# Four edges to a partition instead of three in a graph layer, with places found per load, degrees earlier and chunk sums in free order

## The chip, the cores and the metric

The kernel runs on one core of a Trainium2 chip. The metric is the time of one execution in microseconds (us) on the device; the times shown are of three runs and one further, profiled execution. The engines are named as the profile names them: PE is TensorE (PEld its weight loads), DVE is VectorE, ACT is ScalarE, POOL is GpSimd, SP is SyncE, which here only issues transfers.

## The reference

There are 625 nodes with 512 features and 20,625 edges sorted by destination: 10,000 random ones in both directions and a self loop for each node. Each edge has one of four types and a weight. With layer norms whose gains are applied where named:

```python
h   = maximum(layernorm(x), 0)
msg = sum over r of (h[src] @ W_rel[r] + b_rel[r]) * where(type == r, weight, 0)
agg = segment_sum(msg, dst) / maximum(segment_sum(weight, dst), 1)
x1  = layer_norm(h + h @ W_self + b_self + agg, ln1)
ffn = gelu(x1 @ W_ffn1 + b_ffn1) @ W_ffn2 + b_ffn2       # 512 -> 1024 -> 512
out = x + layer_norm(x1 + ffn, ln2)
```

## The kernel before, in words

The nodes are cut into five blocks of 125. A *table* of 20 chunks, one for each relation and block, holds `h[block] @ W_rel[r]` and, in its 126th row, the relation's bias row; it lies in device memory, and the last nine chunks also stay on chip (`kept`). Blocks 0 to 2 (`OUTER`, the dense blocks) and blocks 3 and 4 (`inner`, the gathered blocks) add up their edges in two different ways.

**Dense blocks.** Every node's edges are consecutive, at most 64 of them (slots). The kernel finds, for each node, where they begin: it compares the first edge of each tile of 128 edges (`find_tiles`, L471), gathers a row of every fourth destination (`dst_4`, an indirect transfer issued by POOL for each block, `rows_of_tiles`, L477), counts in it (`find_windows`, L480) and gathers the 64-slot window (`win`). From the windows come the slots' weights (`slot_weights`, L496), the fields of a slot split into bf16 parts (`slot_fields`, L513), the degrees (`slot_degrees`, `relation_degrees`), and then, for 16 slots at a time (a *unit*, four to a block, twelve in all), one-hot matrices on DVE (`slot_hots`, L608). PE multiplies them into *banks* (`slot_sums`, L637), and DVE reduces each bank into `sums_w` (L643): for each node, a weight for each row of the table. PE then sums the 20 chunks of the table with these weights (`chunk_sum`, L1054); eleven chunks are loaded back, two to a transfer (`chunk_load`), into three buffers `tr`. Six units (`EARLY`) are made during the table's products, the others after them.

**Gathered blocks.** The edges of a part of the list are laid out three to a partition (`EG` = 3): group k holds 128 x 3 edges, and partition p has edges 3p, 3p + 1, 3p + 2 of it. POOL gathers the table row of every edge (`gather`, L931, 128 rows to a transfer) into eight buffers `ms`. ACT scales the first of the three by its weight (`first_row`, L939), DVE adds the others whose destination is the same node (`row_added`, L957), ACT and DVE split the sum in two fp32r parts (`high` L943, `low` L947), and PE adds both with a one-hot of the first edge's node (`edge_sum`, L977 and L978; the last group of a sum in fp32, L980). With EG = 3 there are 23 groups, 69 gathers. A node whose edges begin inside a partition has its first edges there counted apart (`first_edges`, L550, `first_columns`, L565): EG - 1 further gathers for each of the two blocks (`gather_first`, L985, `add_first`, L982).

**Order.** The first part (L815 to L902) has an order written out by hand: a double loop over relation r and block i, and in each turn four matmuls of table rows (`table_rows`, L367) and then the other steps at the turn in which an `if` names them. PE, DVE, ACT and POOL follow it; SP's transfers are placed by the framework, and `later_loads` (L232) gives the weights' loads after each relation. The second part is planned: each step has an engine, a duration, predecessors, buffers and a rank, and `Plan.times` (L103) simulates them and emits in that order. Once emitted, each engine goes strictly in order.

Table products run first, then the self products (`self_part`, L384), chunk sums and gathered sums, then the first norm of a block, its turn (L325), the up product with Gelu (L722, L726), the down product (L740) and the last norm with its store.

Of the kernel before, what the change touches and what calls it, by code (L numbers as in the profile page):

```python
# [14 lines left out]
ALU = mybir.AluOpType  # L15

P = 128
EG = 3
SLOTS = 64
# [119 lines left out]
def gnn_layer(ctx, tc, x, edges, edge_groups, firsts, fourths, windows, w_self, w_rel, w_ffn1, w_ffn2, brel_in, rows_in, bf1_in, out, n_edges):  # L139
# [12 lines left out]
    nc = tc.nc  # L152
# [304 lines left out]

    def before_node(out, of, n):

        nc.vector.tensor_tensor(found[:, :, :n], of, node_f.unsqueeze(2).to_broadcast([P, NB, n]), op=ALU.is_lt)
        nc.vector.reduce_sum(out, found[:, :, :n], axis=mybir.AxisListType.X)

# [11 lines left out]
    def rows_of_tiles(b0, b1):  # L477
        rows_of(fourths, at_i[:, 0, :], lambda b: dst_4[:, b, :], b0, b1)

    def find_windows():  # L480
        n = fourths.shape[1]
        nc.vector.tensor_copy(ends[:, :, :n], dst_4)
        before_node(before[:, 1, :], ends[:, :, :n], n)
        nc.vector.scalar_tensor_tensor(before[:, 1, :], at_f[:, 0, :], float(fourths.shape[1]), before[:, 1, :],
                                       op0=ALU.mult, op1=ALU.add)
        nc.vector.tensor_scalar(at_f[:, 1, :], before[:, 1, :], -1.0, 0.0, op0=ALU.add, op1=ALU.max)
        nc.vector.tensor_copy(at_i[:, 1, :], at_f[:, 1, :])
        rows_of(windows, at_i[:, 1, :], lambda b: win[:, b, :, :].rearrange("p f s -> p (f s)"))

# [106 lines left out]
    QT = 4  # L596
# [213 lines left out]
    CH = 2  # L810
    FIRST_AT = (2, 2)
    units = [(d, u) for d in range(ND) for u in range(SL // UNIT)]
    EARLY = 6
    PER_ROW = 3
    with tc.manual_schedule(engines={PE, DVE, ACT, mybir.EngineType.Pool}):  # L815
        nc.scalar.activation(gelu_of, ones, AF.Gelu)
# [18 lines left out]
        for r in range(R):  # L835
            for i in range(NB):
# [15 lines left out]
                if (r, i) == (0, 0):  # L852
                    rows_of_tiles(0, 2)
                    next_norm(3)
                    rows_of_tiles(2, 4)
                if (r, i) == (0, 1):
                    rows_of_tiles(4, NB)
                if (r, i) == (0, 3):
                    find_windows()
                if (r, i) == (1, 0):  # L860
                    edge_columns()
                    for n in range(NB):
                        nc.vector.tensor_add(xs[:, n, :], xs[:, n, :], b2_bc)
# [15 lines left out]
                if (r, i) == (1, NB - 1):  # L879
                    group_columns()  # L880
# [5 lines left out]
                if (r, i) == FIRST_AT:  # L886
                    first_edges()
                    load_first_edges()
# [6 lines left out]
            later_loads(r)  # L895
        assert not waiting
# [18 lines left out]

    own = {}
    for n, b in enumerate(ep.order):
        first, second, added = self_part(b)
        rank = (2, 0.1 * n) if n < len(OUTER) else (5, n)
        s = op("PE", 1.735, first, take=["ps"], rank=rank)  # L920
        s = op("PE", 1.735, second, after=[s], give=["T"], lag=0.25, rank=rank)
        own[b] = op("DVE", 0.68, added, after=[s], give=["ps"], rank=(0.6,) if b in OUTER else None)
# [130 lines left out]

    def chunk_sum(b, c, first, last):  # L1054
        if first:
            acc[b,] = ps_one.tile([P, D], F32, tag="one", name=f"acc{b}")
        nc.tensor.matmul(acc[b,], sums_w[b][:NG + 1, c, :], kept[(b, c) if (b, c) in kept else c][:NG + 1],  # L1057
                         start=first, stop=last)

# [19 lines left out]

    stay, i = list(range(NC - KEPT, NC)), 0  # L1080
    for d, b in enumerate(OUTER):
        weights_of(d)
        order = (*stay, *range(NC - KEPT))
        for c in order:
            if c not in stay and (b, c) not in here:
# [3 lines left out]
                here.update({(b, c + k): ld for k in range(n)})  # L1089
            first, last = m[b] is None, c == order[-1]  # L1090
            m[b] = op("PE", 0.87, lambda b=b, c=c, first=first, last=last: chunk_sum(b, c, first, last),
                      after=[m[b], here.get((b, c)), summed.get(d)], take=["one"] if first else [],
                      give=["tr"] if (b, c) in here and (c % CH == CH - 1 or c == NC - KEPT - 1) else [], lag=0.25,
                      rank=(2, 2 + 0.01 * i), level=4.4)
            if i == 8:
                t = op("PE", 0.1, lambda: total_outside(), after=[m[b]], take=["ps"], give=["ps"], lag=2.0, rank=(2, 2.085))
            if i == 16:
                op("PE", 0.1, read_outside, after=[t, m[b]], rank=(2, 2.165), level=0.45)
# [209 lines left out]
```

## Time and profile before

| | us |
|---|---|
| three runs | 262.32, 263.18, 266.7 |
| their median | 263.18 |
| profiled execution, time | 264.32 |
| profiled execution, span | 262.4 |
| PE busy | 248.7 (95% of the span) |
| DVE busy | 184.4 (70%) |
| POOL busy | 112.2 (43%) |
| ACT busy | 66.4 (25%) |
| mean transfer rate | 183 GB/s |

The span is what the trace shows from the first instruction to the last; the execution's own time lies 1.9 us above it. All positions below are us from the span's start. A busy PE is not PE at its peak, since the modelled ends of pipelined matmuls overlap the next; the distance from one matmul's start to the next tells more. A fp32 matmul of the source appears as two records. In a timeline, a bracket at a line's end says how long the engine sat idle before it and what ended the wait; "issue" means nothing that the profile shows. Three stretches follow one another: table products to 89, sums and self products to about 153, feed forward mixed with the last sums to 255.6, and then the last norm and store.

### The profile page before, as it was taken

What the parts mean: (1) busy time and instruction counts of PE and PEld (TensorE: products, weight loads), DVE (VectorE), ACT (ScalarE), POOL (GpSimd) and SP (SyncE); (2) the same over time, 40 slices, a digit from 0 to 9 for tenths busy, and PEclk for the clock granted to TensorE, in tenths of its full rate; (3) what the DMA queues carried; (4) which work ended last, traced back from release to release, by engine and by line L of the source; (5) the groups of instructions that cost most, each with busy time, mean ns of one, the idle gap of its engine ahead of it and who ended that gap; (6) DMA issues with size and microseconds to landing.
All of it is one profiled execution on the core that took longest, in us unless ns stands there. A gap on an engine that the chain in (4) does not pass through costs nothing.

```text
span 262.4 us, 3165 instructions
## 1 busy us (share of the span) xinstructions
PE 248.7 (95%) x1047; PEld 141.6 (54%) x1047; DVE 184.4 (70%) x388; ACT 66.4 (25%) x127; POOL 112.2 (43%) x156
## 2 busy tenths in 40 slices
PE   7999998969999999999999999999999999999990
PEld 3444443435555445444445577445559586685960
DVE  4460647699999899962799998697597792711414
ACT  3232111311122202131311043232444532140420
POOL 7163340000400028776876457877778750200100
PEclk9999999999999999999999999999999999999997
DMA  5948863967322287589895679979866651010101
GB/s 207 332 181 256 307 210 109 361 239 297 130 93 65 59 261 210 160 238 283 251 316 190 197 208 251 249 246 258 265 192 170 195 152 42 0 39 0 44 2 40
DMA packets 20259, 47.93 MB, mean 183 GB/s; under 512 B 2383, under 2 KB 3097, under 8 KB 20112
## 3 DMA queue, kind: packets, MB, share of 16 engines
q1 hardware_dynamic: 13636, 27.54, 32.0%
q0 software_dynamic: 6304, 19.89, 26.2%
q10 hardware_dynamic: 300, 0.26, 0.4%
q8 instruction: 9, 0.15, 0.2%
q14 instruction: 10, 0.08, 0.1%
HBM read 41.29 MB, written 6.52 MB: 182 GB/s over the span
## 4 chain that ended last, share of the span: by engine, by line
PE 61%; DVE 23%; DMA 9%; issue 2%; ACT 2%; SPq 1%; DVEq 0%; ACTq 0%
PE pt L372 17%; PE pu L722 14%; PE po L740 13%; PE acc L1057 9%; DVE sums_w L643 5%; DMA table<-m 5%; DVE high L626 4%; DVE low L620 3%; DMA ms<-table,row_i 3%; DVE ea L957 3%; PE bank L637 2%; PE acc L978 1%; DVE eq L623 1%; PE acc L977 1%; SPq L212 1%
## 5 line engine op out<-in xcount | busy, mean ns | idle before, releaser
L933 POOL DMA_INDIRECT ms<-table,row_i x69 | 72.1, 1046 | 52.1 <-DMA tr<-table 26.5
L372 PE MATMUL pt<-wr,hT 128*128 128x512 f32 x160 | 72.0, 599 | 0.0
L372 PEld LDWEIGHTS pt<-wr,hT 128*128 128x128 f32 x160 | 29.7, 193 | 32.0 <-issue 31.1
L722 PEld LDWEIGHTS pu<-x1T,w_sb 128*128 128x128 f32 x320 | 37.7, 192 | 3.4 <-issue 2.4
L722 PE MATMUL pu<-x1T,w_sb 128*128 128x125 f32 x320 | 38.2, 276 | 0.2 <-DVE sums_w L643 0.2
L957 DVE SCALAR_TENSOR_TENSOR ea<-ms,wgt_g,ea 128x512 f32<-128x512 f32 x43 | 31.8, 750 | 8.0 <-DMA ms<-table,row_i 7.6
L740 PE MATMUL po<-w_sb,gT 128*125 128x512 f32 (+2 forms) x96 | 36.0, 521 | 0.0
L1057 PE MATMUL acc<-tr,sums_w 126*128 126x512 f32 x66 | 30.7, 596 | 0.0
L643 DVE TENSOR_REDUCE sums_w<-bank 126x160 f32<-126x480 f32 x48 | 28.7, 651 | 0.8 <-PE bank L637 0.8
L380 ACT ACTIVATE m<-pt,rx 125x512 f32<-125x512 f32 x20 | 13.8, 688 | 57.8 <-PE pt L372 46.4
L939 ACT ACTIVATE ea<-ms,ed 128x512 f32<-128x512 f32 x23 | 15.9, 692 | 45.7 <-DMA ms<-table,row_i 27.4
L1057 PE MATMUL acc<-m,sums_w 126*128 126x512 f32 x54 | 25.7, 600 | 0.0
L726 ACT ACTIVATE gT<-pu,bf 128x125 f32<-128x125 f32 x40 | 14.4, 366 | 38.3 <-PE pu L722 38.3
L637 PEld LDWEIGHTS <-low 128*128 128x128 bf16 x192 | 15.8, 146 | 15.3 <-issue 15.1
L740 PEld LDWEIGHTS po<-w_sb,gT 128*125 128x125 f32 x96 | 16.4, 188 | 14.0 <-issue 11.6
L947 DVE TENSOR_TENSOR el<-ea,eh 128x512 fp32r<-128x512 f32 x20 | 13.6, 685 | 11.1 <-ACT eh L943 11.1
L637 PE MATMUL bank<-high,low 128*128 128x120 bf16 x192 | 15.9, 224 | 3.9 <-DVE sums_w L643 3.9
L943 ACT CAST eh<-ea 128x512 fp32r<-128x512 f32 x20 | 11.7, 584 | 27.3 <-DVE ea L957 24.4
L392 PE MATMUL pz<-ws_sb,hT 128*128 128x512 f32 x40 | 18.3, 596 | 0.0
L748 DVE TENSOR_TENSOR y<-po,z 125x512 f32<-125x512 f32 (+2 forms) x6 | 3.6, 600 | 20.6 <-PE po L740 20.6
L1057 PEld LDWEIGHTS acc<-tr,sums_w 126*128 126x128 f32 x66 | 12.1, 190 | 10.9 <-issue 10.5
L620 DVE TENSOR_TENSOR low<-turned,grid 128x2000 bf16<-128x2000 bf16 x12 | 14.3, 1193 | 3.1 <-ACT turned L606 3.1
(162 smaller groups left out, 232.5 us busy)
## 6 DMA issues: line engine op xcount, KB each, us to landing
tr<-table SPq DMA_DIRECT2D x15, 504.0 KB
table<-m SPq DMA_DIRECT2D x20, 250.0 KB
w_sb<-in_L_gnn_W_ffn_dram SPq DMA_DIRECT2D x2, 2048.0 KB
wr<-in_L_gnn_W_rel_dram SPq DMA_DIRECT2D x3, 1024.0 KB
ms<-table,row_i POOLq DMA_INDIRECT x69, 4.8
ws_sb<-in_L_gnn_W_self_dram SPq DMA_DIRECT2D x1, 1024.0 KB
rows<-in_rows_dram SPq DMA_DIRECT2D x1, 1024.0 KB
out_dram<-y SPq DMA_DIRECT2D x4, 224.0 KB
```

Source lines behind the costliest of these rows:

```text
L372: nc.tensor.matmul(p, hT[i][:, k, :], wr_sb[r][:, k, :], start=(k == 0), stop=(k == KD - 1))
L392: nc.tensor.matmul(p[0], hT[i][:, k, :], ws_sb[:, k, :], start=(k == 0), stop=(k == KD - 1))
L620: nc.vector.tensor_tensor(low[:, :, :NG, :], of[:, 0].rearrange("p (a t) -> p a t", t=TB).unsqueeze(2).to_broadcast([P, nb_, NG, TB]), gri ...
L637: nc.tensor.matmul(p[:, i * W:(i + 1) * W], low[:, t // TB, :, t % TB], high[:, t // TP, :, t % TP], start=True, stop=True)
L643: nc.vector.tensor_reduce(sums_w[OUTER[d]][:NG + 1, :, n0:n0 + 2 * QT].rearrange("p c (t h) -> p t h c", h=2), p[:NG + 1, :QT * 3 * 2 * NC ...
L722: nc.tensor.matmul(pu[:, :nn], w1_sb[:, k, f * P:(f + 1) * P], x1T_b()[:, k, :nn], start=(k == 0), stop=(k == KD - 1))
L726: nc.scalar.activation(box["gT"][:, f, :nn], pus[f][:, :nn], AF.Gelu, bias=bf1[:, f:f + 1])
L740: nc.tensor.matmul(po[h][:n, :w], box["gT"][:, f, at], w2_sb[:, f, c], start=(f == 0), stop=(f == KF - 1))
L933: nc.gpsimd.indirect_dma_start(out=ms[j], out_offset=None, in_=table[:, :], in_offset=bass.IndirectOffsetOnAxis(ap=row_i[:, j:j + 1], axis=0))
L939: nc.scalar.activation(box["sum"], ms[j], AF.Copy, scale=wgt[:, j:j + 1])
L957: nc.vector.scalar_tensor_tensor(to, ms[j], wgt_g[:, k, q - 1:q], box["sum"], op0=ALU.mult, op1=ALU.add)
L1057: nc.tensor.matmul(acc[b,], sums_w[b][:NG + 1, c, :], kept[(b, c) if (b, c) in kept else c][:NG + 1], start=first, stop=last)
```

## The change

`EG` becomes 4: 17 groups of four, 68 gathers, and three first-edge gathers for each gathered block. `find_windows` works on a range of blocks: the dense blocks' places are found in turn (0, 2) from their own `dst_4` rows, the others in (0, 3). The edge columns and the residual adds move to turn (0, 1) and (0, 3); slot weights and fields from (1, 1) to (0, 4); degrees from (2, 0) to (1, 0), group columns from (1, 4) to (1, 1), first edges from (2, 2) to (1, 2), so that all three stand ahead of the first one-hots, which start at (1, 3) instead of (1, 4). Seven units instead of six are made in this part. SP joins the engines that follow the written order, and the later loads are given by turn. In the second part the chunk sums of a block no longer form a chain: any chunk that is there may be next, and the last three self products get a level of their own.

```diff
-EG = 3
+EG = 4
...
-    def later_loads(r):
-        if r == 0:
-            load_wr(2)
+    def later_loads(r, i):
+        if (r, i) == (0, 0):
             bias_rows()
-        if r == 1:
-            load_wr(3)
+        if i == NB - 1 and r < R - 2:
+            load_wr(r + 2)
+        if (r, i) == (1, 2):
+            nc.sync.dma_start(bf1, bf1_in)
             nc.sync.dma_start(ws_sb, w_self.rearrange("(k p) n -> p k n", p=P))
             load_rows(rows[:, :4 * D], 0, 4 * D)
             load_rows(rows[:, 5 * D:], 5 * D, 6 * D)
-            nc.sync.dma_start(bf1, bf1_in)
-        if r == 2:
+        if (r, i) == (2, 1):
             nc.sync.dma_start(w1_sb, w_ffn1.rearrange("(k p) f -> p k f", p=P))
+        if (r, i) == (3, 0):
             nc.sync.dma_start(w2_sb, w_ffn2.rearrange("(k p) n -> p k n", p=P))
...
-    FIRST_AT = (2, 2)
+    FIRST_AT = (1, 2)
-    EARLY = 6
+    EARLY = 7
-    with tc.manual_schedule(engines={PE, DVE, ACT, mybir.EngineType.Pool}):
+    with tc.manual_schedule(engines={PE, DVE, ACT, mybir.EngineType.Pool, mybir.EngineType.SP}):
...
                 if (r, i) == (0, 0):
                     rows_of_tiles(0, 2)
                     next_norm(3)
-                    rows_of_tiles(2, 4)
+                    rows_of_tiles(2, ND)
                 if (r, i) == (0, 1):
-                    rows_of_tiles(4, NB)
+                    rows_of_tiles(ND, NB)
+                    edge_columns()
+                    for n in range(2):
+                        nc.vector.tensor_add(xs[:, n, :], xs[:, n, :], b2_bc)
+                if (r, i) == (0, 2):
+                    find_windows(0, ND)
                 if (r, i) == (0, 3):
-                    find_windows()
-                if (r, i) == (1, 0):
-                    edge_columns()
-                    for n in range(NB):
+                    find_windows(ND, NB)
+                    for n in range(2, NB):
                         nc.vector.tensor_add(xs[:, n, :], xs[:, n, :], b2_bc)
-                if (r, i) == (1, 1):
+                if (r, i) == (0, 4):
                     slot_weights(0, ND)
                     slot_fields()
-                if (r, i) == (2, 0):
+                if (r, i) == (1, 1):
+                    group_columns()
+                if (r, i) == (1, 0):
                     slot_weights(ND, NB)
                     slot_degrees()
                     degrees_turned = relation_degrees()
...
-                if (r, i) >= (1, 4) and waiting and len(later) + len(sums_now) <= UNIT // QT:
+                if (r, i) == FIRST_AT:
+                    first_edges()
+                    load_first_edges()
+                if (r, i) >= (1, 3) and waiting and len(later) + len(sums_now) <= UNIT // QT:
...
+    OWN_LEVEL = 4.35
-        rank = (2, 0.1 * n) if n < len(OUTER) else (5, n)
+        rank, level = ((2, 0.1 * n), None) if n < len(OUTER) else ((5, n), OWN_LEVEL)
...
-        order = (*stay, *range(NC - KEPT))
-        for c in order:
+        begun = op("PE", 0.0, None, after=[m[OUTER[d - 1]] if d else None, summed.get(d)], take=["one"], rank=(2, 2 + 0.01 * i), level=0)
+        parts = []
+        for c in range(NC):
+            loaded = c < NC - KEPT
...
-                      after=[m[b], here.get((b, c)), summed.get(d)], take=["one"] if first else [],
+            s_ = op("PE", 0.87, lambda b=b, c=c: chunk_sum(b, c),
+                    after=[begun, ld if loaded else None, parts[-1] if loaded and c % CH else None],
...
+        m[b] = op("PE", 0.0, None, after=parts, lag=0.25, level=0)
```

More of the change, by code (lines that the diff above doesn't have):

```diff
@@ L885, in gnn_layer @@
                         nc.vector.tensor_scalar(g_bc, g_bc, 1.0 / RS, None, op0=ALU.mult)
-                if (r, i) == FIRST_AT:
-                    first_edges()
-                    load_first_edges()
+                later_loads(r, i)
                 if (r, i) == (3, 2):
@@ L1052, in chunk_load, with chunk_sum @@
         nc.sync.dma_start(t[:NG + 1, :n, :], table[c * P:(c + n) * P, :].rearrange("(k p) d -> p k d", p=P)[:NG + 1])
-    def chunk_sum(b, c, first, last):
-        if first:
+    done = {b: 0 for b in OUTER}
+    def chunk_sum(b, c):
+        if not done[b]:
             acc[b,] = ps_one.tile([P, D], F32, tag="one", name=f"acc{b}")
+        done[b] += 1
         nc.tensor.matmul(acc[b,], sums_w[b][:NG + 1, c, :], kept[(b, c) if (b, c) in kept else c][:NG + 1],
-                         start=first, stop=last)
+                         start=done[b] == 1, stop=done[b] == NC)
     m, ld, t, here = {b: None for b in OUTER}, None, None, {}
@@ L1078, in weights_of @@
             summed[d] = e
-    stay, i = list(range(NC - KEPT, NC)), 0
+    i = 0
     for d, b in enumerate(OUTER):
         weights_of(d)
-        order = (*stay, *range(NC - KEPT))
-        for c in order:
-            if c not in stay and (b, c) not in here:
+        begun = op("PE", 0.0, None, after=[m[OUTER[d - 1]] if d else None, summed.get(d)], take=["one"], rank=(2, 2 + 0.01 * i), level=0)
+        parts = []
+        for c in range(NC):
+            loaded = c < NC - KEPT
+            if loaded and c % CH == 0:
                 n = min(CH, NC - KEPT - c)
@@ L1088, in gnn_layer @@
                         rank=(0, i))
-                here.update({(b, c + k): ld for k in range(n)})
-            first, last = m[b] is None, c == order[-1]
-            m[b] = op("PE", 0.87, lambda b=b, c=c, first=first, last=last: chunk_sum(b, c, first, last),
-                      after=[m[b], here.get((b, c)), summed.get(d)], take=["one"] if first else [],
[L1093 to L1098, printed above, removed]
+            s_ = op("PE", 0.87, lambda b=b, c=c: chunk_sum(b, c),
+                    after=[begun, ld if loaded else None, parts[-1] if loaded and c % CH else None],
+                    give=["tr"] if loaded and (c % CH == CH - 1 or c == NC - KEPT - 1) else [], lag=0.25,
+                    rank=(2, 2 + 0.01 * i), level=4.4)
+            parts.append(s_)
+            if d == 0 and c == NC - 4:
+                t = op("PE", 0.1, lambda: total_outside(), after=[s_], take=["ps"], give=["ps"], lag=2.0, rank=(2, 2.085))
+                t = op("PE", 0.1, read_outside, after=[t], rank=(2, 2.165), level=4.6)
             i += 1
+        m[b] = op("PE", 0.0, None, after=parts, lag=0.25, level=0)
     for b in OUTER:
```

27 lines of the change are left out of this document (12 added, 15 removed).

## The prediction

> **What bounds the kernel now.** I read the busy time of the engines in stretches first, then TensorE's timeline where a stretch is not full, then VectorE's and GpSimd's timelines for what stands behind the gaps. Columns of the stretches: from:to, length, then busy time of PE, PEld, DVE, ACT, POOL, the granted clock, DMA share, GB/s.
>
> ```profile
> 45.00:60.00 15.00, 12.36 (x49) 6.45 (x49) 11.86 (x34) 3.47 (x6) 0.00 (x0) 1.00 0.84 294
> 60.00:89.30 29.30, 29.30 (x140) 15.58 (x139) 27.79 (x70) 5.88 (x10) 3.07 (x9) 1.00 0.36 128
> 89.30:130.00 40.70, 39.89 (x128) 18.53 (x126) 32.19 (x54) 9.10 (x16) 26.26 (x34) 1.00 0.77 219
> 130.00:153.00 23.00, 21.90 (x114) 12.60 (x113) 22.74 (x41) 3.41 (x7) 14.88 (x18) 1.00 0.77 244
> 153.00:255.60 102.60, 102.59 (x511) 69.10 (x509) 63.67 (x109) 33.46 (x72) 50.88 (x65) 1.00 0.50 142
> ```
>
> The reader should see that TensorE sets the end: from 153 on it never waits, and before that it idles, most of all from 45 to 60. So an edit pays only by taking matmuls away or by closing TensorE's gaps. The gaps lie at 42.7 (turning the slot fields) and 56.0 (the first banks):
>
> ```profile
> 42.73 0.81 PE L603 MATMUL tf<-ident_b,fields 128*128 128x128 bf16 x3
> 44.84 7.11 PE L372 MATMUL pt<-wr,hT 128*128 128x512 f32 x16
> 56.02 0.41 PE L637 MATMUL bank<-high,low 128*128 128x120 bf16 x4
> 58.92 0.41 PE L637 MATMUL bank<-high,low 128*128 128x120 bf16 x4 [2.48 <-DVE sums_w L643]
> 59.73 1.51 PE L372 MATMUL pt<-wr,hT 128*128 128x512 f32 x3
> 89.32 5.37 PE L392 MATMUL pz<-ws_sb,hT 128*128 128x512 f32 x12
> ```
>
> The price of the same work unhindered comes from the chain that ended last (start, us, what): a table row's eight matmul records 3.44, three banks 0.74, five turns 0.28, one fp32r matmul of the gathered sums 0.23 to 0.24, a block's up products 7.14.
>
> ```profile
> 64.09 3.44 PE pt L372 x8
> 67.53 0.74 PE bank L637 x12
> 72.49 0.28 PE tf L603 x5
> 155.32 0.24 PE acc L977
> 155.56 0.23 PE acc L978
> 241.79 7.14 PE pu L722 x64
> ```
>
> So the turns lose 44.84 - 42.73 - 0.28 = 1.83 us and the banks 59.73 - 56.02 - 0.74 = 2.97, together 4.80. Between 89.3 and 153 another 0.81 + 1.10 = 1.9 us is idle, in small pieces. Both large gaps are VectorE's lateness:
>
> ```profile
> 27.96 0.32 DVE L482 CAST ends<-dst 128x160 f32<-128x160 int32 x1 [10.36 <-DMA dst<-in_fourths_dram,at_i]
> 29.51 0.41 DVE L428 CAST fl<-ed 128x486 f32<-128x486 int32 x1
> 32.18 3.14 DVE L863 TENSOR_TENSOR xs<-xs,rows 128x512 f32<-128x512 f32 x5
> 38.73 0.35 DVE L499 CAST ends<-win 128x192 f32<-128x192 int32 x1 [3.41 <-DMA win<-in_windows_dram,at_i]
> 44.13 0.56 DVE L528 TENSOR_TENSOR fields<-found,fields 128x384 bf16<-128x384 f32 x1
> 47.76 1.20 DVE L620 TENSOR_TENSOR low<-turned,grid 128x2000 bf16<-128x2000 bf16 x1 [3.07 <-ACT turned L606]
> 50.61 0.20 DVE L587 TENSOR_TENSOR wgt_g<-fl 128x46 f32<-128x46 f32 x1
> 51.80 0.22 DVE L499 CAST ends<-win 128x128 f32<-128x128 int32 x1
> 55.37 1.19 DVE L620 TENSOR_TENSOR low<-turned,grid 128x2000 bf16<-128x2000 bf16 x1
> 64.44 0.17 DVE L463 TENSOR_TENSOR found<-ends,node_f 128x20 f32<-128x20 f32 x1
> 65.75 1.22 DVE L643 TENSOR_REDUCE sums_w<-bank 126x160 f32<-126x480 f32 x2
> 88.99 1.23 DVE L643 TENSOR_REDUCE sums_w<-bank 126x160 f32<-126x480 f32 x2 [0.79 <-PE bank L637]
> ```
>
> VectorE sleeps 10.36 us until all five `dst` gathers have landed, then 3.41 more for `win`; from 47.76 to 90.1 it has almost no gap. That stretch is VectorE's as much as TensorE's.
>
> **The change, part by part.**
>
> *Places found per load.* The norms end at 27.96 - 10.36 = 17.6. In the sleep now stand the edge columns (32.18 - 29.51 = 2.67) and two of the five residual adds (3.14 x 2/5 = 1.26): 21.5. The GpSimd rows, and the landings of the third `dst` gather alone and of all `win` gathers:
>
> ```profile
> 18.14 1.00 POOL L468 DMA_INDIRECT dst<-in_fourths_dram,at_i  x1 [0.18 <-issue]
> 29.87 0.95 POOL L468 DMA_INDIRECT win<-in_windows_dram,at_i  x1 [7.71 <-DVE at_i L487]
> 32.50 1.19 POOL L468 DMA_INDIRECT win<-in_windows_dram,at_i  x1 [0.30 <-issue]
> ```
> ```profile
> DMA to landing us min/median/max: 3.0/3.0/3.0
> ```
> ```profile
> DMA to landing us min/median/max: 5.9/6.4/6.8
> ```
>
> The third lands at 18.14 + 3.0 = 21.1, so VectorE does not wait. Finding the places took 29.51 - 27.96 = 1.55 for five blocks; at the same price for three, 23.1. The third `win` gather is issued at 23.2 + 2.63 = 25.9 (spacing 1.32) and is usable 38.73 - 32.50 = 6.23 later: 32.1 instead of 38.73. Below, its wait could be the 3.0 of the `dst` gather, since the loads of W_self and the bias rows (1 MB each) leave this window; above, it is 6.8. I take 6.23. The last two places and three adds fit in that wait. Weights and fields took 44.69 - 38.73 = 5.96, so they end at 38.1. TensorE's turns come one row earlier, at 42.73 - 3.44 = 39.3: the 1.83 us stall goes.
>
> *Degrees ahead of the one-hots.* Next late is the first one-hot set, since degrees (55.37 - 51.80 = 3.57), group columns (51.80 - 50.61 = 1.19) and first edges (65.75 - 64.44 = 1.31) now stand before it: 38.1 + 6.07 = 44.2, and with the set (50.61 - 47.76 = 2.85) 47.0. TensorE arrives at 39.3 + 0.28 + 2 x 3.44 = 46.5, since the banks follow one row sooner as well. It waits 0.5; with the upper `dst` and `win` waits some 3.
>
> *Seventh unit early.* It adds 2.85 + 4 x 0.61 (half of the pair at 65.75) = 5.3 us of VectorE work and four banks (1.0 us of TensorE) before the end of the table rows. VectorE: 38.1 + (90.1 - 47.76 - 0.79) + 5.3 = 85.0; its own waits there are 29.30 - 27.79 = 1.5: 86.5. TensorE: 89.32 - 4.80 + 1.0 + 0.5 = 86.0. The last banks wait for the sums, so I take 86.5. TensorE is then 89.32 - 86.5 = 2.8 us ahead with 1.0 us of later work done: **-3.8 us**.
>
> *Loads on SP.* The order is now written out. The stores of m_0 to m_7, on which the three `msg` buffers hang, no longer queue behind W_self and the bias rows:
>
> ```profile
> ACT m L380 <- DMA table<-m: 11.5, 3, 4.9
> ```
>
> Four PSUM buffers hide these waits from TensorE, so I cost them at nothing beyond the earlier turn copies already counted. W_ffn2 (2 MB) moves to just before the last four stores. At 219 GB/s (first gather stretch) it takes 9.6 us; issued near 69, behind the first store of the last relation, it is through by 79, before the last store near 85.5. If not, the gathers start later, not TensorE. The Trainium skill, page DMA: Bandwidth & Descriptors, section Queues, rings and completion order, says that each DMA engine takes a ring's descriptors in order: the stores cannot pass W_ffn2. By that rule taken alone the gathers' start would move by at most the part of those 9.6 us that lies after 85.5, here none; no row of this case shows the new order.
>
> *Four edges to a partition.* 23 groups become 17. Each group that needs no special end costs TensorE two fp32r matmuls: 6 x (0.24 + 0.23) = **-2.8 us**, all on the path. VectorE:
>
> ```profile
> L957 DVE SCALAR_TENSOR_TENSOR ea<-ms,wgt_g,ea 128x512 f32<-128x512 f32 x43 | 31.8, 750 | 8.0 <-DMA ms<-table,row_i 7.6
> L947 DVE TENSOR_TENSOR el<-ea,eh 128x512 fp32r<-128x512 f32 x20 | 13.6, 685 | 11.1 <-ACT eh L943 11.1
> ```
>
> It has five adds more (51 for 46) and two more for the first rows: 7 x 0.75 = 5.3 up, 6 x 0.69 = 4.1 down. ScalarE loses six scalings and six casts, off the path. GpSimd issues 68 + 6 = 74 gathers instead of 73. What may cost: eight gather buffers now hold two groups, not nearly three.
>
> *Chunk sums in free order, later self products.* No instruction is added. The best is the 1.9 us of idle between 89 and 153; the worst I put at 2 us of waits for a chunk load whose cover of kept rows is now split. I take 0: one-hot sets still meet the four `ps` buffers there.
>
> Sum: -3.8 - 2.8 = -6.6. The profiled execution spans 262.4 and took 264.32; its span becomes 255.8 and its time 257.7. The median of the runs is 263.18, 1.1 under that execution: **256.6 us**.
>
> **The rivals.**
>
> *A, the gathers become the bound (the slower side).* First and last gather and TensorE's last use:
>
> ```profile
> 96.01 0.96 POOL L933 DMA_INDIRECT ms<-table,row_i  x1 [26.53 <-DMA tr<-table]
> 212.10 0.96 POOL L933 DMA_INDIRECT ms<-table,row_i  x1 [0.16 <-issue]
> 221.17 1.02 PE L980 MATMUL acc<-es,oh 128*128 128x512 f32 x2
> ```
>
> The pace is (212.10 - 96.01) / 72 = 1.61 us. With a start at 93.2 and 73 steps the last gather goes at 210.9; landing, three adds and the wait between engines (about 6.5, an estimate) give 217.4. In the changed order TensorE has after it the ups and downs of blocks 2 and 4, 2 x (7.14 + 2 x 3.44) = 28.0, and its own two records and four turns, some 1.4; its end would be 255.6 - 6.6 = 249.0, so it needs them at 219.6. The margin is 2.2 us: it begins to cost at a pace of 1.64, the kernel is slower than before at 1.73, slower by 2% at 1.80. For it: a buffer is now held for three adds in a row, VectorE is full from 130 to 153, and two groups fill all buffers. Against it: VectorE has one unit less to do there, and before the change the same stop occurred without costing TensorE anything. At 1.70 the time would be 261.
>
> *B, no gain in the first 90 us.* The `win` gathers or the first one-hots come so late that a stall of the old size stands at the banks: only the matmuls are saved, 260.4.
>
> *C, every stall goes.* -4.80 - 2.8 - 1.9: 253.7.
>
> **How the numbers follow.** Forecast 0.52 (254.8 to 258.6), A 0.20 (258 to 270, half of it above 263.2, a third above 268.4), B 0.18, C 0.10. The likeliest gives 256.6. A measurement tells about 2% from no change: under 257.9 is faster, over 268.4 slower. Under 257.9 lie C, most of the forecast and little else: 0.56; over 268.4 the third of A: 0.07; between, 0.37. The range goes from 253.0 (C) to 262.5 (B and the lower half of A).
>
> **What would show it.** Right: the turns near 39 with no gap, a gap under 1 us at the first banks, the self products starting near 86.5, the first gather near 93, 14 pairs of fp32r matmuls, no TensorE idle from 150 on. Wrong: a gap of 3 us at the first banks (B); TensorE idle before the gathered sums after 150, with GpSimd's gathers waiting on VectorE's adds (A); TensorE waiting for chunk loads; the first gather no earlier than 96, which would say W_ffn2 held the stores.

## The result, and the profile after

| | before | after |
|---|---|---|
| executions | 12 | 12 |
| median, lowest, highest (us) | 262.5, 261.81, 266.7 | 261.07, 256.49, 263.83 |
| profiled execution: time, span | 264.32, 262.4 | 259.54, 257.7 |

The ratio after to before is 0.9865, 95% interval 0.9825 to 0.9905: 3.5 us faster (1.35%), which is less than the 2% that counts as faster. The forecast was 256.6; the median lies 4.5 us above it and inside the range. The ratio leaves out executions more than 1.5% above the kernel's own fastest, which is half of those of the changed kernel (they scatter over 7.3 us); the medians over all executions give 0.9946.

In the changed kernel TensorE's timeline (start, us, the idle time before it in brackets, then what ended it) shows the first 90 us as forecast, or better:

```profile
39.15 0.44 PE L601 MATMUL tf<-ident_b,fields 128*128 128x128 bf16 x5
46.35 0.92 PE L635 MATMUL bank<-high,low 128*128 128x120 bf16 x12
85.44 5.37 PE L390 MATMUL pz<-ws_sb,hT 128*128 128x512 f32 x12
...
123.17 0.51 PE L979 MATMUL acc<-eh,oh 128*128 128x512 f32 x1 [1.20 <-ACT eh L945]
130.36 1.12 PE L1062 MATMUL acc<-m,sums_w 126*128 126x512 f32 x2 [1.02 <-DVE z L994]
138.44 1.98 PE L1062 MATMUL acc<-tr,sums_w 126*128 126x512 f32 x4 [1.47 <-DMA tr<-table]
...
221.04 1.02 PE L982 MATMUL acc<-es,oh 128*128 128x512 f32 x2
```

The turns start at 39.15 and the first banks at 46.35, neither with a gap, and the self products at 85.44 instead of 89.32. But between 120 and 140 there are waits that were not there before: for a gathered sum, for the `z` that frees an accumulator, and for a chunk load. And the last gathered sum runs at 221.04, where it ran at 221.17 before: a lead of 3.9 us at the self products is 0.1 us there. The kernel still ends sooner, since less is left after that sum: 36.2 us from the start of its last matmul (257.7 less 221.5), where it was 40.8 (262.4 less 221.6).

The same in stretches (from:to, length, busy time of PE, PEld, DVE, ACT, POOL, granted clock, DMA share, GB/s), the kernel before first:

```profile
0.00:90.00 90.00, 84.82 (x303) 41.76 (x304) 63.60 (x177) 20.79 (x36) 20.20 (x40) 1.00 0.59 206
118.00:155.00 37.00, 35.44 (x154) 19.17 (x152) 30.36 (x53) 8.15 (x14) 24.75 (x32) 1.00 0.81 246
155.00:230.00 75.00, 75.00 (x345) 48.02 (x344) 56.23 (x96) 25.12 (x53) 48.51 (x63) 1.00 0.65 182
```

and the kernel after:

```profile
0.00:90.00 90.00, 88.31 (x328) 44.04 (x329) 72.79 (x198) 21.20 (x36) 20.27 (x40) 1.00 0.62 215
118.00:155.00 37.00, 33.09 (x148) 17.60 (x148) 31.26 (x55) 5.88 (x10) 19.13 (x27) 1.00 0.87 242
155.00:230.00 75.00, 74.83 (x373) 49.96 (x372) 53.42 (x91) 22.25 (x51) 48.44 (x62) 1.00 0.61 178
```

Idle time is length less PE's busy time. It fell from 5.18 to 1.69 up to 90, rose from 1.56 to 3.91 from 118 to 155, and from 155 to 230 there is next to none in either. Over the whole span TensorE stands 13.9 us (257.7 less 243.8 busy) where it stood 13.7 (262.4 less 248.7): the idle time taken out of the first 90 us came back later, and what is gone is 4.9 us of busy time, not all of it saved matmuls, since the ends of matmuls are modelled. GpSimd's timeline tells what the gathers did with their earlier start:

```profile
91.48 1.28 POOL L935 DMA_INDIRECT ms<-table,row_i  x1 [44.89 <-PE bank L635]
...
146.57 0.95 POOL L935 DMA_INDIRECT ms<-table,row_i  x1 [10.29 <-DVE ea L959]
...
213.80 1.50 POOL L935 DMA_INDIRECT ms<-table,row_i  x1 [0.17 <-issue]
```

They begin at 91.48 instead of 96.01 and end at 213.80 instead of 212.10: a pace of (213.80 - 91.48) / 73 = 1.68 us instead of 1.61. They stop once for 10.29 us (the longest such stop before was 3.27, at 150.01), because VectorE adds no gathered row between 128.89 and 145.55; it is at the third dense block's one-hots and sums then:

```profile
128.89 0.75 DVE L959 SCALAR_TENSOR_TENSOR ea<-ms,wgt_g,ea 128x512 f32<-128x512 f32 x1 [1.41 <-ACT ea L941]
...
135.71 1.19 DVE L618 TENSOR_TENSOR low<-turned,grid 128x2000 bf16<-128x2000 bf16 x1
...
139.78 1.19 DVE L618 TENSOR_TENSOR low<-turned,grid 128x2000 bf16<-128x2000 bf16 x1
...
143.29 2.35 DVE L641 TENSOR_REDUCE sums_w<-bank 126x160 f32<-126x480 f32 x4 [0.25 <-PE bank L635]
...
145.55 0.75 DVE L959 SCALAR_TENSOR_TENSOR ea<-ms,wgt_g,ea 128x512 f32<-128x512 f32 x1
```

### The profile page after: what moved, and what is told of

Read it like the earlier page. It is cut to its first block, busy times and chain, and to the rows that moved or that the text cites. A ratio compares the mean times of both kernels' runs of the same rounds, so it can differ in the third digit from the quotient of the medians.

```text
span 257.7 us, 3133 instructions
## 1 busy us (share of the span) xinstructions
PE 243.8 (95%) x1035; PEld 138.7 (54%) x1035; DVE 185.8 (72%) x393; ACT 59.0 (23%) x115; POOL 109.7 (43%) x155
## 4 chain that ended last, share of the span: by engine, by line
PE 72%; DMA 11%; POOL 6%; DVE 5%; issue 3%; ACT 1%; POOLq 0%; DVEq 0%; ACTq 0%
PE pt L370 27%; PE acc L1062 12%; PE pu L720 12%; PE po L738 11%; POOL ms L935 5%; DMA tr<-table 5%; DMA ms<-table,row_i 5%; PE bank L635 4%; PE pz L390 2%; DMA xs<-in_x_dram 1%; PE tp_h L323 1%; PE acc L982 1%; PE acc L980 1%; PE acc L979 1%; DVE z L994 1%
## 5 line engine op out<-in xcount | busy, mean ns | idle before, releaser
L935 POOL DMA_INDIRECT ms<-table,row_i x68 | 68.7, 1010 | 76.9 <-PE bank L635 44.9
L959 DVE SCALAR_TENSOR_TENSOR ea<-ms,wgt_g,ea 128x512 f32<-128x512 f32 x48 | 35.7, 750 | 14.2 <-DMA ms<-table,row_i 12.5
L720 PEld LDWEIGHTS pu<-x1T,w_sb 128*128 128x128 f32 x320 | 37.0, 192 | 1.9 <-issue 1.4
L720 PE MATMUL pu<-x1T,w_sb 128*128 128x125 f32 x320 | 37.2, 275 | 0.0
L1062 PE MATMUL acc<-tr,sums_w 126*128 126x512 f32 x66 | 31.6, 598 | 1.5 <-DMA tr<-table 1.5
L738 PEld LDWEIGHTS po<-w_sb,gT 128*125 128x125 f32 x96 | 16.4, 188 | 13.9 <-issue 11.4
L941 ACT ACTIVATE ea<-ms,ed 128x512 f32<-128x512 f32 x17 | 11.8, 692 | 48.1 <-DMA ms<-table,row_i 40.0
L949 DVE TENSOR_TENSOR el<-ea,eh 128x512 fp32r<-128x512 f32 x14 | 9.6, 685 | 9.7 <-ACT eh L945 9.7
L635 PE MATMUL bank<-high,low 128*128 128x120 bf16 x192 | 15.3, 225 | 1.0 <-DVE sums_w L641 1.0
L624 DVE TENSOR_TENSOR high<-eq,turned 128x640 bf16<-128x640 bf16 x36 | 15.6, 487 | 0.4
L1062 PEld LDWEIGHTS acc<-m,sums_w 126*128 126x128 f32 x54 | 9.8, 190 | 11.2 <-issue 9.1
```

The costliest lines, as they stand in the source:

```text
L624: nc.vector.tensor_mul(high[:, :, a * 2 * NC:(a + 1) * 2 * NC, :], eq, pairs(2 + a))
L635: nc.tensor.matmul(p[:, i * W:(i + 1) * W], low[:, t // TB, :, t % TB], high[:, t // TP, :, t % TP], start=True, stop=True)
L720: nc.tensor.matmul(pu[:, :nn], w1_sb[:, k, f * P:(f + 1) * P], x1T_b()[:, k, :nn], start=(k == 0), stop=(k == KD - 1))
L738: nc.tensor.matmul(po[h][:n, :w], box["gT"][:, f, at], w2_sb[:, f, c], start=(f == 0), stop=(f == KF - 1))
L935: nc.gpsimd.indirect_dma_start(out=ms[j], out_offset=None, in_=table[:, :], in_offset=bass.IndirectOffsetOnAxis(ap=row_i[:, j:j + 1], axis=0))
L959: nc.vector.scalar_tensor_tensor(to, ms[j], wgt_g[:, k, q - 1:q], box["sum"], op0=ALU.mult, op1=ALU.add)
```

## The experiments

Three parts are told apart: P, the edits of the first 90 us (places, degrees, seventh unit, SP's order); E, four edges to a partition; F, the chunk sums in free order with the inner blocks' self products at `OWN_LEVEL`. Ratios are to the kernel before, run on the same chip, with 95% intervals; different rows can come from different chips.

| run | parts | ratio | interval |
|---|---|---|---|
| eg4_alone | E | 0.9973 | 0.9942 to 1.0005 |
| early_alone | P | 0.9980 | 0.9950 to 1.0011 |
| two_parts | P, E | 0.9955 | 0.9912 to 0.9998 |
| after | P, E, F | 0.9865 | 0.9825 to 0.9905 |
| free_alone | free order only | 1.0359 | 1.0281 to 1.0438 |
| chained_sums | P, E, own level only | 1.0088 | 1.0047 to 1.0128 |
| eg3_again | P, F | 1.0129 | 1.0028 to 1.0230 |
| own_mid | P, E, F with level 4.45 | 0.9950 | 0.9906 to 0.9994 |
| no_chunk_loads | after without chunk loads | 0.9844 | 0.9777 to 0.9910 |
| before_no_loads | before without chunk loads | 0.9908 | 0.9871 to 0.9945 |
| no_pause | after, no GpSimd pauses | 1.0662 | 1.0571 to 1.0753 |
| plan_late | after, other planner figures | 1.0021 | 0.9987 to 1.0054 |
| kept12 | after, fewer chunk loads | 0.9898 | 0.9847 to 0.9949 |

### One part at a time

**eg4_alone**, in the kernel before:

```diff
-EG = 3
+EG = 4
```

> The kernel before with EG = 4 and nothing else. Theory J (the chunk sums' free order puts chunk loads and gathers on the DMA engines at the same time, and the stalls of 120 to 140 come from that): the six sums saved on TensorE, 6 x 0.47 = 2.8 us, are had in full, 259.7 us beside 262.5, and TensorE's idle time from 120 to 140 stays at the 0.8 us of before. Rival G (four gathers to a sum make each sum late, whatever the order of the chunk sums): the same stalls as in the changed kernel, 2 us or more from 120 to 140, and 262 to 263 us.

Measured: 0.9973, that is 0.7 us where 2.8 was expected (interval -0.1 to 1.5). The first row is VectorE's first one-hot set in the kernel before, the second the same in this kernel, the third group is TensorE here. The code up to these rows is the same in both.

```profile
47.76 1.20 DVE L620 TENSOR_TENSOR low<-turned,grid 128x2000 bf16<-128x2000 bf16 x1 [3.07 <-ACT turned L606]
```
```profile
45.25 1.20 DVE L620 TENSOR_TENSOR low<-turned,grid 128x2000 bf16<-128x2000 bf16 x1 [1.28 <-ACT turned L606]
```
```profile
56.44 0.41 PE L637 MATMUL bank<-high,low 128*128 128x120 bf16 x4 [0.72 <-DVE sums_w L643]
...
86.85 3.65 PE L392 MATMUL pz<-ws_sb,hT 128*128 128x512 f32 x8
...
184.44 0.63 PE L325 MATMUL tp_x<-ident,x 128*128 128x128 f32 x4 [1.40 <-DVE x L688]
```

Two things follow. E's matmuls are saved, but TensorE then stands elsewhere, as at 184.44; from 120 to 140 it stands 1.68 us, between theory J's 0.8 and rival G's 2. And the wait at the first banks, 2.48 us in the profiled execution of before, is 0.72 here, and the self products start at 86.85 instead of 89.32, though all that E does there is to widen a few of VectorE's small operations. The two other kernels with the old first 90 us agree, free_alone above and before_no_loads below:

```profile
45.55 1.20 DVE L620 TENSOR_TENSOR low<-turned,grid 128x2000 bf16<-128x2000 bf16 x1 [1.28 <-ACT turned L606]
```
```profile
87.99 2.36 PE L392 MATMUL pz<-ws_sb,hT 128*128 128x512 f32 x5
```

So the profiled execution of before had a wait on ScalarE's turn copy of 3.07 us that three others had at 1.3. ScalarE's rows tell why, before first and then eg4_alone:

```profile
42.65 0.69 ACT L380 ACTIVATE m<-pt,rx 125x512 f32<-125x512 f32 x1 [4.88 <-DMA table<-m]
46.23 0.69 ACT L380 ACTIVATE m<-pt,rx 125x512 f32<-125x512 f32 x1 [2.89 <-DMA table<-m]
46.82 0.84 ACT L606 COPY turned<-tf 64x320 bf16<-64x320 bf16 x2
```
```profile
42.57 0.69 ACT L380 ACTIVATE m<-pt,rx 125x512 f32<-125x512 f32 x1 [2.48 <-PE pt L372]
44.30 0.85 ACT L606 COPY turned<-tf 64x320 bf16<-64x320 bf16 x2 [1.04 <-PE tf L603]
```

In before, ScalarE stood until the store of an earlier table row (`table<-m`) had left its buffer, and the copy stood behind it in ScalarE's order; in eg4_alone it was TensorE's turns that ScalarE waited for. In the changed kernel ScalarE waits for no store (11.5 us in all before). The 1.8 us are as large as the distance of this execution from the median (264.32 less 262.5), which does not show that they make it.

**early_alone**, the kernel before with P:

```diff
-    FIRST_AT = (2, 2)
+    FIRST_AT = (1, 2)
-    EARLY = 6
+    EARLY = 7
...
-                if (r, i) == (0, 3):
-                    find_windows()
+                if (r, i) == (0, 2):
+                    find_windows(0, ND)
...
```

> The kernel before with the edits of the first 90 us alone (places on their own loads, degrees ahead, seventh unit early, SP's order). On the record these were to bring 3.8 us. Theory O: self products start near 86 as in the changed kernel and the lead is kept to the end: 258.7 beside 262.5. Theory D: the lead is lost between 107 and 140, 261.5 or more.

Measured: 0.9980, that is 0.5 us and not 3.8. The self products start at 85.64, and from 118 to 155 it stands 3.35 us; its stretch and the waits in it:

```profile
118.00:155.00 37.00, 33.65 (x159) 19.37 (x158) 30.32 (x52) 8.23 (x15) 21.68 (x29) 0.95 0.78 226
```
```profile
122.38 0.50 PE L979 MATMUL acc<-eh,oh 128*128 128x512 f32 x1 [1.47 <-ACT ea L941]
...
135.56 0.41 PE L635 MATMUL bank<-high,low 128*128 128x120 bf16 x4 [1.07 <-DVE sums_w L641]
```

This agreed with theory D as far as it goes: from 118 to 155 idle time is 3.35 us instead of the 1.56 of before, and the granted clock there is 0.95 instead of 1.00. The waits shown are for VectorE and ScalarE, not for a chunk load. **two_parts** (P and E) answers to the product of the two, 0.9980 x 0.9973 = 0.9953. Its edit, against the changed kernel and in part:

```diff
-        rank, level = ((2, 0.1 * n), None) if n < len(OUTER) else ((5, n), OWN_LEVEL)
+        rank, level = (2, 0.1 * n) if n < len(OUTER) else (5, n), None
...
+        order = (*stay, *range(NC - KEPT))
```

> Four edges and the edits of the first 90 us; the chunk sums in the order of before, and the inner blocks' self products with the rank of before (behind all else, so that they fill gaps). Theory O (with their own level all 24 products run at once near 96, and nothing is left to fill TensorE when gathers and chunk loads come late): products lie at 101, 115 and 127 again as in the run with four edges alone, TensorE idle from 120 to 140 falls from the 5.1 us of the run with chained sums to 2 or less, 258 us or less. Theory D (gathers and chunk loads ask for more than the DMA engines move from 107 to 136, because all starts 4 to 5 us sooner): idle stays at 3.5 us or more, 261 us or more.

Measured: 0.9955. Self products lie at 114, 118 and 127 again, yet TensorE stands 3.49 us from 118 to 155. From 120 to 140 it is 2.68, between theory O's 2 and theory D's 3.5; the median, 262.52, is what D asked for.

### The free order

**free_alone**: the kernel before with the free order but no level for the self products. **chained_sums**: the changed kernel with the old order, the level left in:

```diff
-        for c in range(NC):
+        order = (*stay, *range(NC - KEPT))
+        for c in order:
...
-                    after=[begun, ld if loaded else None, parts[-1] if loaded and c % CH else None],
+                      after=[m[b], here.get((b, c)), summed.get(d)], take=["one"] if first else [],
```

> The kernel before with the free order of the chunk sums alone. Theory J: TensorE's idle time in the 40 us from the first gather's landing rises from about 1.5 to 4 us, time 264 to 266 beside 262.5. Rivals G and S: within 1 us of 262.5, since neither the groups nor the start has changed.

> The changed kernel with the chunk sums in the order of before (the kept chunks first, each sum behind the one before it). Theory J: first chunk load used near 110 instead of 105.9, TensorE idle from 120 to 140 falls from 3.9 us to 1.5 or less, the 10.3 us gap in the gathers at 136 goes, time 258 or less. Rivals G and S: the idle time stays at 3 us or more, and the time at 260.5 to 262.

Measured: 1.0359 and 1.0088. Theory J is wrong: with the old order the changed kernel is slower, not faster, and TensorE stands 5.79 us from 118 to 155 instead of 3.91. In free_alone TensorE does not wait for transfers: it stands 0.25 us in the 40 us behind 96, where J had 4. Sixteen of the self products' matmuls are left to 193.83, and what is added to their result waits with them:

```profile
193.83 7.03 PE L392 MATMUL pz<-ws_sb,hT 128*128 128x512 f32 x16
...
210.56 2.04 PE L974 MATMUL acc<-brel,deg_T 4*128 4x512 f32 x2 [8.34 <-DVE z L992]
```

Each half of F costs time without the other (the free order was tried without P and E only). Together they are worth 0.9865 / 0.9955 = 0.991, about 2.4 us; the intervals leave 0.8 to 4, and the medians over all executions, 0.9946 and 0.9966, only 0.5. What they move is the end of the sums over loaded chunks; two_parts first, then after (durations, then first and last start):

```profile
L1059 PE MATMUL acc<-tr,sums_w x66: 590/592/697, 106.7 to 192.7; 126*128 126x512 f32 x66
```
```profile
L1062 PE MATMUL acc<-tr,sums_w x66: 590/592/697, 105.9 to 176.2; 126*128 126x512 f32 x66
```

The last one starts 16 us sooner, so more of the dense blocks' feed-forward can run ahead of the last gathered sum: after it 40.3 us are left in two_parts (261.0 less 220.7, the start of its last matmul) and 36.2 in the changed kernel (257.7 less 221.5). This is read from the two traces; no run tests it.

**eg3_again** (`EG = 3` in the changed kernel):

> The changed kernel with EG = 3. Theory J: the six sums come back, +2.8 us, some 263.5 to 264 beside 261.07, and TensorE still stands 3 us or more from 120 to 140. Rival G: the stalls go (under 1.5 us from 120 to 140) and the time is 261 or less. Rival S (all that starts 4 us sooner reaches a stretch whose end the transfers set): the stalls stay, and the time is within 1 us of the changed kernel's.

Measured: 1.0129 in only four executions. E, worth 0.7 us alone, is worth 1.0129 less 0.9865, about 7 us, here (the intervals leave 4 to 10, the medians over all executions 5). The waits are not E's (3.53 us from 118 to 155), so G falls, and rival S's 1 us falls with the time. Why E is worth more here than alone is open.

**own_mid** (`OWN_LEVEL = 4.45`):

> The changed kernel with OWN_LEVEL = 4.45: the chunk sums go ahead of the inner blocks' self products, so the first loaded chunk is used near 96 instead of 105.9 and the loads are spread over ten more microseconds. Theory D: less is asked of the DMA engines from 109 to 136, idle from 120 to 140 2 us or less, 259 or less, if no self product is left so late that sums wait for it (two are still in the order behind the chunk sums). Theory O: the products now lie behind and fill gaps, the same sign. If both fall: 261 or more.

Measured: 0.9950. Idle time from 118 to 155 fell to 1.72, and 2.76 us appeared from 90 to 118, when the chunk sums come first. The stall moved, and the median of 262.78 is past the 261 at which theories D and O were both to fall.

### Is it the transfers?

**no_chunk_loads** and **before_no_loads** leave out the chunk loads; the sums are taken over a kept chunk, so they are of other data.

```diff
-        t = edge.tile([P, CH, D], F32, tag="tr", name=f"tr_{b}_{c}", bufs=LA)
-        kept.update({(b, c + k): t[:, k, :] for k in range(n)})
-        nc.sync.dma_start(t[:NG + 1, :n, :], table[c * P:(c + n) * P, :].rearrange("(k p) d -> p k d", p=P)[:NG + 1])
+        kept.update({(b, c + k): kept[NC - KEPT + (c + k) % KEPT] for k in range(n)})
```

> The changed kernel with the 18 chunk loads left out, their sums taken over a chunk that is kept in SBUF (the sums are of other data, the order and number of instructions elsewhere the same). Theory D: without these 8.3 MB the gathers land in time, TensorE stands under 1 us from 120 to 140, the 10.3 us gap in the gathers goes, 255.5 or less with all clocks at 0.993 or more. Theory O: the wait on a chunk (1.5 us at 136) goes, the waits on gathered sums (1.2 and 1.0 us) stay, 258 or more.

> The kernel before with its 18 chunk loads left out in the same way (sums over a chunk kept in SBUF). Theory D (the jam of gathers and chunk loads between 107 and 140 takes the lead of the changed kernel): the kernel before hardly pays for the loads, so it gains little by losing them, 261.5 to 263 where the kernel before stands at 262.5 to 263.4; beside 259.0 for the changed kernel without loads the lead would then be some 3.5 to 4 us. Rival N (the loads cost both kernels the same): 260.5 or less, and the lead of the changed kernel without its loads is the 1.3% that it has with them.

The changed kernel without its loads: two stretches, the longest stop of its gathers, and what TensorE waits for behind 155:

```profile
118.00:155.00 37.00, 36.96 (x168) 20.62 (x168) 32.96 (x58) 6.12 (x12) 23.36 (x29) 1.00 0.46 136
155.00:230.00 75.00, 72.08 (x353) 47.41 (x352) 49.75 (x84) 20.49 (x48) 45.29 (x59) 1.00 0.48 141
```
```profile
143.25 0.96 POOL L935 DMA_INDIRECT ms<-table,row_i  x1 [6.07 <-DVE ea L959]
```
```profile
177.49 5.42 PE L738 MATMUL po<-w_sb,gT 128*125 128x512 f32 x12 [1.08 <-ACT gT L724]
...
194.66 1.16 PE L720 MATMUL pu<-x1T,w_sb 128*128 128x125 f32 x8 [0.74 <-ACT gT L724]
```

The stalls of 118 to 155 go entirely (0.04 us), so in this kernel they hang on the chunk loads; whether on their bytes or on the waits for them, this run cannot tell. The gathers' stop shrinks from 10.29 us to 6.07 and does not go. But 2.9 us of idle time come up behind 155, and the time, 0.9844, is hardly below the 0.9865 with the loads. The kernel before gains 0.9% by the same cut, although its profiled execution then stands 2.67 us from 118 to 155, more than the 1.56 with the loads. So theory D was right on the place and wrong on the price: without loads the lead of the changed kernel is 0.9844 / 0.9908 = 0.9935, not the 3.5 to 4 us that D had. The intervals leave room for rival N's 1.3%, which is not shown. **kept12** takes away a quarter of the bytes:

```diff
-    KEPT = 9
+    KEPT = 12
-    ES = 6
-    LA = 3
-    CH = 2
+    ES = 5
+    LA = 4
+    CH = 1
```

> The changed kernel with 12 chunks kept in SBUF instead of 9 (24 chunk reads of 252 KB instead of 33, 6.0 MB instead of 8.3 MB), paid for by loads of one chunk with four buffers instead of two chunks with three, and by one edge-sum buffer less. If the chunk loads' bytes beside the gathers make the stalls of 118 to 155 (3.9 us with all loads, 0.04 us with none), a quarter fewer bytes take about a quarter to a half of them: idle 2 to 3 us there, and a time 1 to 2 us below the changed kernel's, ratio to the kernel before 0.978 to 0.984. If the gathers' own chain is what limits (as the run without loads hints, which stood 2.9 us after 155), the idle time moves behind 155 and the ratio stays at 0.985 to 0.99. If single-chunk loads come too late for lack of buffers: idle over 4 us and a ratio over 0.99.

Measured: 0.9898, idle 2.66 us from 118 to 155 (in the expected range) and no gain beside the changed kernel, whose interval it overlaps (0.978 to 0.984 was expected). The idle time did not move behind 155 either (0.34 us up to 230). Its one large stall, 2.50 us for the `z` that frees an accumulator, is followed by some 3.4 us at half the clock.

### The pace of gathers and the plan

**no_pause** (`RUN = 1000` for 4, so that no memsets stand between the gathers, in the planner's account neither) and **plan_late**:

```diff
-    LAND = 4.5
+    LAND = 7.0
-                ld = op("SP", 0.3, ..., take=["tr"], lag=8.0, order=True,
+                ld = op("SP", 0.3, ..., take=["tr"], lag=12.0, order=True,
```

> The changed kernel without the two memsets after every fourth gather (about 1.25 us each time on GpSimd). Theory D: no gain, since the transfers and not GpSimd's issue set when rows land: 261 or more. Rival P (GpSimd's pace of 1.57 us a gather makes the sums late): the waits from 120 to 130 go and the time falls by 2 us or more, 259 or less.

> The changed kernel with other figures in its planner: 7.0 us instead of 4.5 for the landing of a gather, 12 instead of 8 for that of a chunk load. No work and no byte is changed, only the order written out. Theory D, with the addition that an order planned for early rows is what makes TensorE and VectorE stand: sums are placed later, other work before them; idle from 120 to 140 falls from 3.9 to 2 us or less, median 258.5 or less, and the runs lie closer together (3 us instead of 7). If the transfers alone set the pace whatever the order: idle 3 us or more, 260.5 or more.

GpSimd in no_pause:

```profile
117.91 0.95 POOL L935 DMA_INDIRECT ms<-table,row_i  x1 [0.30 <-issue]
121.81 0.95 POOL L935 DMA_INDIRECT ms<-table,row_i  x1 [2.95 <-issue]
...
134.73 0.95 POOL L935 DMA_INDIRECT ms<-table,row_i  x1 [3.14 <-DVE mv_z L303]
...
216.92 0.97 POOL L935 DMA_INDIRECT ms<-table,row_i  x1 [0.30 <-issue]
```

It issues 21 gathers in a row, most of them 1.26 us apart, then stands, and ends at 216.92, later than with the pauses (213.80): rival P is wrong, issuing faster does not bring the gathers to their end sooner. TensorE's order was then planned for a pace that does not come, and the median is 280.06. Since this edit changes the pace and the plan at once, it doesn't tell how much each costs. In plan_late, where only the plan changes, idle time from 118 to 155 fell from 3.91 to 1.80 as expected, but 4.31 us came up from 155 to 230; the ratio is 1.0021, and the median 263.79 where 258.5 or less was expected:

```profile
118.00:155.00 37.00, 35.20 (x192) 22.03 (x192) 31.38 (x54) 8.06 (x17) 21.14 (x29) 1.00 0.78 231
155.00:230.00 75.00, 70.69 (x304) 42.96 (x303) 52.98 (x91) 18.08 (x40) 46.73 (x61) 1.00 0.62 182
```

By the ratios, no run that does all the work beats the changed kernel.

## Why the prediction was right or wrong

**Places, degrees: right.** No gap at the turns (39.15; forecast 39.3) nor at the first banks (46.35; forecast 46.5 with 0.5 us of waiting), self products at 85.44 (forecast 86.5), first gather at 91.48 (forecast near 93). Rival B is out, and W_ffn2 did not hold the stores.

**What they are worth: wrong, in two steps.** The term was -3.8 us; early_alone gives -0.5 (interval -1.3 to +0.3). The first step that failed is the sentence "So the turns lose ... 1.83 us and the banks ... 2.97, together 4.80." It took both stalls from one execution, in which VectorE waited 3.07 us for a turn copy; in three others with the same code it waited 1.3, and in the two of them whose TensorE rows are shown the self products start at 86.85 and 87.99 instead of 89.32. Against those the lead is about 1.4 to 2.5 us, not 3.9. The prediction saw that this execution stood 1.1 us above the median (1.8 with more executions) and moved its baseline by that, but subtracted the stall in full. If that excess is the stall, the same microseconds were counted twice; this is not shown, and the next step speaks against it. The second step that failed is the unspoken one that a lead at the self products lasts to the end. Most of it was given back as new idle time between 118 and 155, where TensorE waits for VectorE, ScalarE and a chunk load.

**Loads on SP: right.** The stores no longer hold ScalarE: its waits for `table<-m` went from 11.5 us to none, and that is what made the copy late in the profiled execution of before.

**Four edges, -2.8 us: right as TensorE's work, wrong as time.** All 14 pairs are there (`acc<-eh,oh` counts 14), yet alone it brings 0.7 us (interval -0.1 to 1.5): TensorE then waits for what it reaches sooner. The words "all on the path" failed.

**Free order, 0: too low by the ratios, though within its bounds of -1.9 to +2 once the interval is taken in.** By the ratios it brings about 2.4 us and is the largest of the three; by the medians over all executions it is 0.5, so its size is not settled. Its two edits were priced together as one that adds no instruction; each alone costs time.

The sum by the ratios is -0.5 - 0.7 - 2.4 = -3.6, beside the measured -3.5. That is no confirmation, since the last term is what the other two leave. The forecast of -6.6 was right in sign and made of other terms: 3.1 us of its distance of 4.5 lie here. For the rest, the median of the changed kernel lies 2.1 us above the 259.0 that the ratio gives, and the baseline was 0.7 too high (263.18 from three executions, 262.5 from twelve), which made the forecast 0.7 too high too. The range holds because it is 9.5 us wide, and because a term put at 0 made up for part of two that were too large, which is luck. What the prediction held likeliest, a time under 257.9 (0.56), did not come.

**Rival A** showed its signs on GpSimd, but not its cost. The pace is 1.68, past the 1.64 from which it was to cost, with the last gather at 213.80 where the forecast had 210.9, and in the longest stop GpSimd waits for VectorE's adds. But TensorE was to stand behind 150, before the last sum, and from 155 to 230 it stands 0.17 us. It stands before the fourth sum, at 123.17, which is ahead of GpSimd's stop, and at the chunk load at 138.44. Without the chunk loads GpSimd still stops 6.07 us and TensorE stands 0.04 us there. So the last sum, at 221.04, is late against its 219.6 although no idle time stands beside it: TensorE lost its time before 155.

**What stays open.** TensorE's last gathered sum starts at 219.6 to 221.2 in before, early_alone, eg4_alone, two_parts, no_chunk_loads and after alike, whether the first gather goes at 96.0 or at 90.0. A late gather does not hold it there directly, since in none of them TensorE is idle just before it. What else makes the starts so alike is not shown; other orders move it (224.63 in plan_late, 234.11 in free_alone). Nor is it shown why the store that held ScalarE landed late in the one execution of before.

## What to carry to other kernels

Before a stall is written into the sum as a gain, see whether it is there in full in other executions: when the profiled one lies above the median, the excess may be that very stall. TensorE busy 95% of the span does not make its time additive: here taking away 2.8 us of matmuls, or 2 us of early stall, brought 0.5 to 0.7 us each, and the traces show new waits behind each, in an order that is fixed beforehand. What paid most, by the ratios, was an edit that adds no work and lets the order put something else there, and only with both of its halves. When a wait differs between executions, follow the engine that ended it one step back: here ScalarE's copy was late because of a store ahead of it in ScalarE's own order.

## What the hardware showed beyond that

A short stall can cost twice. In own_mid TensorE waits 1.52 us at 112.5, and 0.8 us after it starts again the granted clock falls to half for 3.4 us (stretches of one microsecond, the clock third from the right):

```profile
112.00:113.00 1.00, 0.51 (x2) 0.00 (x0) 0.00 (x0) 0.22 (x1) 0.31 (x1) 1.00 1.02 295
113.00:114.00 1.00, 0.00 (x0) 0.00 (x0) 0.00 (x0) 0.98 (x2) 0.26 (x1) 1.00 0.95 332
114.00:115.00 1.00, 0.73 (x2) 0.42 (x3) 0.98 (x2) 0.00 (x0) 0.70 (x2) 0.93 0.95 361
115.00:116.00 1.00, 1.00 (x2) 0.54 (x2) 0.96 (x2) 0.00 (x0) 1.00 (x2) 0.50 0.81 246
116.00:117.00 1.00, 1.00 (x3) 0.34 (x1) 0.95 (x3) 0.01 (x1) 0.49 (x2) 0.50 0.76 221
117.00:118.00 1.00, 1.00 (x3) 0.48 (x2) 0.39 (x1) 1.00 (x2) 0.97 (x1) 0.50 0.60 201
118.00:119.00 1.00, 1.00 (x4) 0.46 (x3) 1.00 (x3) 0.17 (x1) 0.70 (x1) 0.86 0.33 70
```

By these rows that is an estimated 1.7 us of work lost (3.4 us at half speed). In eg3_again a wait of 2.12 us, which ends at 140.33, did not lower the clock, so the length of one wait doesn't decide it. The Trainium skill, page TensorE: Matmul & The Clock Gate, section What's actually happening, has the clock fall to half after at least one idle window of about 3.4 us and return after as much activity; the return agrees with these rows, the fall does not, since here TensorE was busy for 1.2 of the 3 us before it.

The changed kernel's twelve executions had a mean granted clock of 0.988, 78 of the kernel before, on the chips of the experiments, 0.993. Among the twelve the longer spans go with the lower clocks (262.0 us at 0.980, 257.7 at 0.996, though the shortest, 254.7, had 0.993; correlation of span and lost clock 0.81). An estimate from these figures is that 0.005 x 259 = 1.3 us of the gain may be lost this way. That stalls make the lower clocks of the longer executions is not shown: only the profiled execution, at 0.996, has a trace.
